# A four-layer image network on one core: the third layer's spectrum layout, token statistics, skip terms and tail rearranged

## The chip, the core and the metric

The kernel runs on one core of one Trainium2 chip. Its metric is the device time of that core in microseconds, from start to end of one launch. The core has four compute engines that work side by side, each through its own list of instructions in order: TensorE (PE; its weight loads are listed as PEld), VectorE (DVE), ScalarE (ACT) and GpSimd (Pool). SyncE (SP) issues the transfers between the chip's memory (HBM) and the core's buffer (SBUF), also in order. TensorE writes its results to PSUM. Engines wait for one another through semaphores.

## What is computed

A batch of four images, each 64 x 64 positions with 128 channels, passes four layers of the form x = x + f(gn(x)), where gn is a group normalisation. The first is a selective scan, the second a Fourier convolution, the fourth a neighbourhood attention; they are not changed. The third is cut here to what matters. It takes each image as t = 64 tokens of H x W = 64 x 128 numbers, and every instance_norm is over one token:

```python
def instance_norm(x, g, b):
    mu = jnp.mean(x, axis=(-2, -1), keepdims=True)
    var = jnp.var(x, axis=(-2, -1), keepdims=True)
    return (x - mu) * jax.lax.rsqrt(var + EPS) * g[:, None, None] + b[:, None, None]

tokens_norm = instance_norm(tokens, norm1_g, norm1_b)
k = fno_layer(tokens_norm, key_w, ..., (Hs, Ws))
q = fno_layer(tokens_norm, query_w, ..., (Hs, Ws))
v = fno_layer(tokens_norm, value_w, ..., (H, W))
...
attn = fno_layer(attn, proj_w, proj_skip_w, proj_skip_b, (H, W))
attn = instance_norm(attn + tokens, attn_norm_g, attn_norm_b)
m = instance_norm(attn, norm2_g, norm2_b)
m = fno_layer(m, mixer_w1, ..., norm=(mixer_norm_g1, mixer_norm_b1), act=_gelu)
m = fno_layer(m, mixer_w2, ..., norm=(mixer_norm_g2, mixer_norm_b2))
out = instance_norm(m, mixer_out_g, mixer_out_b) + attn
```

An fno_layer is a product of a few low Fourier coefficients with weights (norm of that, if one is given) plus a pointwise skip of its input. After the layer, x (its input) is added to out.

## The kernel before

Every image of the third layer lies in SBUF as tiles of 128 partitions x 32 columns j x 128 numbers. A column j holds two tokens, 64 lines each, on the partitions. So a token statistic is one bn_stats per j on DVE (over the 128 numbers of a line) and small TensorE products (in_pm, with the matrices tok and tokM) that sum over the 64 lines.

`layer2` (line 1408) runs the four images through the generator `layer2_image` (line 949), two at a time. `Pace` (line 884) is a planner: it issues the instructions of both images in the order that its own costs give, through `in_turn` (line 922), each generator running until its next `yield`. The order that results is kept on PE, ACT, DVE and Pool; SP takes its transfers in the order of issue. All instructions of the layer are recorded under the planner's call, line 914, so one tells them apart by their tiles.

The large tiles (`xg`, `U2`, `Z2`, `ti`, `z`, `m`, `sp`) share a pool of seven buffers, handed round among both images; a new tile waits for the last reader of the tile whose buffer it takes.

The stages of an image, with the tiles by which the trace names them:

1. Load `xg`, group statistics (`pg`, `gn_st`), normalise, store to a scratch in HBM; token statistics (`in_st`, `in_pm`).
2. The front. `dft_y` (line 1018) transforms the columns: TensorE's `pu`, which ACT copies from PSUM to `U` (line 1025). `U` is the tile `U2`, laid out as token column, real or imaginary component, frequency or row: [P, 64, 2, 32]. Then `px` (line 1139) takes one slice of `U` for each of 32 rows and 2 components as weights, with `quad` as the moving data; `pv` reads eight or fewer rows of `U` as moving data, ACT copies it to `V`, and `pG` (line 1176) multiplies slices of `V` by themselves. Each matrix product of the program has two records in the trace.
3. Attention scores: `TT`, `Z` (two DVE operations and one on Pool per part, three parts), `psc`, softmax in `Sc`, transposed to `PT`; then `pk` applies the value weights to the image in another order of tokens (`ti`), which is written to HBM and read back as `z` (line 1277).
4. `pz`: the two images of a pair meet, and a product with streamed weights (`wr`, `WX`) gives the spectrum `Zp` of both.
5. `synthesis` (line 1029): TensorE's `pa`, an ACT copy to `S`, TensorE's `pb` and then a given `put` for each block of four columns. Here `put` adds to `z` on DVE. When all blocks are done, 32 bn_stats per image read `z` (`token_stats`, line 966), and the factors `sa`, `za`, `A1`, `A2`, `B1` follow.
6. Mixer 1, `spectral` (line 1333): `dft_y` of `z`, `pq` (quad as weights, `U` as moving data), DVE's `Zp` (a product with the mixer weights), synthesis with `put` an ACT copy to `sp`. In the same time DVE makes `m` = `z` x `A2`. Then 32 bn_stats on `sp`, factors `q1` and `f1`, m = gelu(sp x q1 + f1 + m), half of it on ACT and half on DVE.
7. Mixer 2: the same on `m`, into a new `sp`, with 32 bn_stats.
8. The tail: sp x q2, m = m x scal(10) + sp (`stt`, line 1388), x loaded anew into `sp`; 32 bn_stats on `m`; then, per chunk of eight columns, z x sa + f3 on ACT, m x q3 on DVE, the sums with `sp` and `z` on DVE and the store.

`by_rows` (line 1014) is a DVE product or sum of eight columns with one number per partition and column, `affine` (line 1004) is eight ACT instructions of one column each.

Of the kernel before, what the change touches and what calls it, by code (L numbers as in the profile page):

```python
# [17 lines left out]
P = 128  # L18
Q = 68
# [864 lines left out]
class Pace:  # L884


    def __init__(self, nc):
        self.nc, self.free, self.t, self.first = nc, {}, 0.0, None

    def spend(self, name, op, out):  # L890
        n = 1
        for d in out.shape[1:]:
            n *= d
        fixed, each, land = {
            "tensor": (0.02, 0.0017, 0.1),
            "vector": (0.07, 0.00104, 0.1),
            "scalar": (0.17, 0.00083, 0.1),
            "gpsimd": (0.1, 0.0023, 0.1),
            "sync": (0.1, 0.0, 2.0 + n * out.shape[0] * 4e-5),
        }[name]  # L900
        end = max(self.free.get(name, 0.0), self.t) + fixed + each * n
        self.free[name] = end
        self.first = self.first or name
        self.t = end + land

# [43 lines left out]
def layer2_image(sh, w, pools, x_in, x_out, scr, wt, parity, beside):  # L949
# [16 lines left out]
    def token_stats(src):  # L966


        st = own([P, NJ, 6], "in_st")
        for j in range(NJ):  # L970
            nc.vector.bn_stats(st[:, j, :], src[:, j, :])
            if j % 8 == 7:
                yield j == NJ - 1
# [12 lines left out]
        yield True  # L986
        return pm[:, 0, :], pm[:, 1, :]
# [29 lines left out]

    def dft_y(src):

        U = large("U2", [P, 64, 2, 32])  # L1020
        for g in range(NJ // 4):
            pu = ps.tile([P, 4, P], F32, name="pu", tag="a")
            for q in range(4):
                nc.tensor.matmul(pu[:, q, :], lhsT=src[:, 4 * g + q, :], rhs=w["an"], start=True, stop=True)
            nc.scalar.copy(U[:, 8 * g : 8 * g + 8].rearrange("p t q r -> p (t q r)"), pu.rearrange("p q m -> p (q m)"))
            yield g == 7
        return U

    def synthesis(Z, put):
# [20 lines left out]
        for g0 in range(0, 16, 4):  # L1050
            S_next = columns(g0 + 4) if g0 < 12 else None
            for u in range(2):
                pb = ps.tile([P, 4, DM], F32, name="pb", tag="b")
                for q in range(2):
                    nc.tensor.matmul(
                        pb,
                        lhsT=w["bd"][64 * u : 64 * u + 64, q, :],
                        rhs=S[64 * u : 64 * u + 64, :, q, :],
                        start=(q == 0),
                        stop=(q == 1),  # L1060
                    )
                put(u, g0, pb)
            S = S_next
            yield g0 == 12

    def at(t, u, g0):
        return t.rearrange("p (g u) c -> p u g c", u=2)[:, u, g0 : g0 + 4, :]
# [66 lines left out]
    for g in range(8):  # L1134
        px = ps.tile([64, 4, Q], F32, name="px", tag="b")
        for e in range(4):
            for q in range(2):
                nc.tensor.matmul(
                    px[:, e, :], lhsT=U[:, :, q, 4 * g + e], rhs=w["quad"][:, q, :], start=(q == 0), stop=(q == 1)
                )  # L1140
        nc.scalar.activation(Xs[0:64, 4 * g : 4 * g + 4, :], px, AF.Copy, scale=scT[:64])
        if g == 0:
# [22 lines left out]
    for v, r0, r1 in ((1, 0, 8), (2, 8, 9), (0, 9, 16), (3, 16, 17), (0, 17, 24), (1, 24, 32), (None, 0, 0)):  # L1165
        nr = r1 - r0
        if nr:
            V = tmp.tile([66, 64, 8], F32, name="V2", tag="S2", bufs=3)
            pv = ps.tile([66, 64, nr], F32, name="pv", tag="a")
            for q in range(2):  # L1170
                nc.tensor.matmul(pv, lhsT=w["gram"][:, v, q, :], rhs=U[:, :, q, r0:r1], start=(q == 0), stop=(q == 1))
            nc.scalar.copy(V[:, :, :nr], pv)
        if V_last is not None:
            for e in range(V_last[1]):
                Ve = V_last[0][:, :, e]
                nc.tensor.matmul(pG, lhsT=Ve, rhs=Ve, start=(n_done == 0), stop=(n_done == 31))
                n_done += 1
        V_last = V, nr
# [151 lines left out]
    ts(B1, B1, scal(7), scal(9), ALU.add, ALU.add)  # L1330
    yield False

    def spectral(src, mix):
        U = yield from dft_y(src)
        Zm = own([Q, 64, 32], "Zp", tmp)
        for g in range(4):
            px = ps.tile([Q, 16, 32], F32, name="pq", tag="b")
            for q in range(2):
                nc.tensor.matmul(
                    px, lhsT=w["quad"][:, q, :], rhs=U[:, 16 * g : 16 * g + 16, q, :], start=(q == 0), stop=(q == 1)  # L1340
                )
            tt(Zm[:, 16 * g : 16 * g + 16, :], px, mix.unsqueeze(1).to_broadcast([Q, 16, 32]), ALU.mult)
            yield g == 3
        sp = large("sp")
        yield from synthesis(Zm, lambda u, g0, p: nc.scalar.copy(at(sp, u, g0), p))
        return sp


    m = large("m")
    for c in range(4):  # L1350
        by_rows(m, z, A2, c, ALU.mult)
    yield False
    sp = yield from spectral(z, w["mix1"])
    mu, var = yield from token_stats(sp)
    vs = col("vs")
    tt(vs, A1, A1, ALU.mult)
    tt(vs, vs, var, ALU.mult)
# [18 lines left out]
        yield c == 4  # L1376


    sp = yield from spectral(m, w["mix2"])
    mu, var = yield from token_stats(sp)  # L1380
# [10 lines left out]
    mu, var = yield from token_stats(m)  # L1391
    q3 = yield from norm_scale(var, 14, "q3")
    f3 = minus_mean(mu, q3, "f3")
    ts(f3, f3, scal(15), None, ALU.add)
    tt(f3, f3, za, ALU.add)
    yield True
    for n, c in enumerate(C4):
        rows = slice(1024 * n, 1024 * n + 1024)
        affine(z, z, sa, f3, n)
        by_rows(m, m, q3, n, ALU.mult)  # L1400
        tt(m[:, c, :], m[:, c, :], sp[:, c, :], ALU.add)
        yield False
        tt(m[:, c, :], m[:, c, :], z[:, c, :], ALU.add)
        nc.sync.dma_start(x_out[rows, :].rearrange("(j p) d -> p j d", p=P), m[:, c, :])
        yield n == 3

# [467 lines left out]
```

## Time and profile before

| what | us |
|---|---|
| median of the runs | 8041.62 |
| lowest and highest of 3 runs | 8036.29, 8046.07 |
| the profiled execution | 8031.55 |
| its span in the trace | 8029.5 |
| PE busy (share of the span) | 6458.9 (80%) |
| DVE busy | 6721.0 (84%) |
| ACT busy | 6138.5 (76%) |
| Pool busy | 5478.0 (68%) |

The span is the time from the first to the last instruction that the profiler recorded on the core; the profiled execution's own time lies a little above it. Most of the busy time belongs to the first layer, so the shares say little on the third. This is how that layer looks among the costliest groups of instructions (line, engine, operation, tile written and tiles read, shapes and count, then busy us and mean ns of one, then idle time of the engine ahead of the group and what ended it), taken over the window from 6380 to 7480 us:

```profile
L914 PE MATMUL pb<-S,bd 64*128 64x512 f32 x384 | 99.3, 612 | 0.0
L914 PE MATMUL px<-quad,U 128*64 128x68 f32 x512 | 59.6, 284 | 1.4 <-ACT U L914 1.4
L914 ACT COPY U<-pu 128x512 f32<-128x512 f32 x96 | 55.5, 584 | 79.7 <-PE pu L914 79.5
L914 DVE BATCH_NORM_STATS2 in_st<-sp 128x6 f32<-128x128 f32 x256 | 53.5, 277 | 31.6 <-ACT sp L914 31.6
L914 ACT ACTIVATE z<-z,f,sa 128x128 f32<-128x128 f32 x128 | 50.1, 480 | 5.7 <-DVE f L914 5.7
L914 PE MATMUL pG<-V 66*64 66x64 f32 x256 | 36.3, 307 | 0.0
```

Instructions of one engine overlap in their latency, so the mean of one can be longer than the step from one start to the next; of a chain of equal records, the length divided by the count is that step. 128x512 reads as 128 partitions and 512 elements each.

### The profile page before, as it was taken

Reading aid. Unit: us, or ns where it says so; the run is one execution under the profiler, and the core shown is the slowest. Engines: PE = TensorE matmul, PEld = TensorE weight load, DVE = VectorE, ACT = ScalarE, POOL = GpSimd, SP = SyncE. Lnnn points to the kernel's source line nnn. Section 1 sums busy time; section 2 is a strip of 40 time slices with the busy share of each in tenths; the row PEclk is TensorE's granted clock in tenths of the full one; section 3 lists DMA queues with packets and bytes.
Section 4 is the critical chain, followed back from the end, with each engine's and each line's share of the span. In section 5 each row is a group of like instructions: output and inputs, shape, how many; then the busy total and the mean of one; then the engine's idle time right before and its main releaser. Section 6 shows DMA issues by size and latency. Waiting matters only on the chain.

```text
span 8029.5 us, 141288 instructions
## 1 busy us (share of the span) xinstructions
PE 6458.9 (80%) x52976; PEld 4085.6 (51%) x52976; DVE 6721.0 (84%) x7948; ACT 6138.5 (76%) x9798; POOL 5478.0 (68%) x2502
## 2 busy tenths in 40 slices
PE   7688888778888877888887777787778878687789
PEld 3344554444455444445544444454457666464456
DVE  2899999999999999999999999999945545645778
ACT  3799999989999898999999999999822213315567
POOL 0899999998998898899989999999900010020233
PEclk9899999999999999999999999999989978798899
DMA  6446555545655554565655445555542141331332
GB/s 121 163 153 191 170 178 179 161 161 160 193 179 179 173 171 166 164 186 176 185 179 176 161 158 185 176 176 178 174 96 56 42 109 31 90 104 31 105 93 80
DMA packets 1403839, 1165.69 MB, mean 145 GB/s; under 512 B 759829, under 2 KB 1197681, under 8 KB 1336210
## 3 DMA queue, kind: packets, MB, share of 16 engines
q1 hardware_dynamic: 1401474, 1154.93, 46.7%
q8 instruction: 417, 6.83, 0.4%
q14 instruction: 268, 2.20, 0.1%
q10 hardware_dynamic: 1680, 1.74, 0.1%
HBM read 962.66 MB, written 189.74 MB: 144 GB/s over the span
## 4 chain that ended last, share of the span: by engine, by line
PE 35%; ACT 26%; DVE 22%; issue 9%; POOL 4%; DMA 4%; SPq 1%; DVEq 0%; ACTq 0%; POOLq 0%
DVE h L531 13%; ACT hT L401 9%; ACT dA L530 9%; PE pt L391 7%; PE cv L215 6%; PE yT L426 4%; POOL dB L525 2%; ACT e L480 2%; PE po L726 1%; PE pf L721 1%; PE pz L914 1%; PE pt L1557 1%; PE pu L914 1%; DVE in_st L914 1%; ACT delta L333 1%
## 5 line engine op out<-in xcount | busy, mean ns | idle before, releaser
L531 DVE TENSOR_TENSOR_SCAN h<-dA,state,dB 128x512 f32<-128x512 f32 x4096 | 4920.3, 1267 | 219.7 <-POOL dB L525 104.1
L525 POOL TENSOR_TENSOR dB<-du,Bb 128x1024 f32<-128x1024 f32 x2048 | 4808.3, 2385 | 335.7 <-DVE h L531 209.9
L391 PE MATMUL pt<-ident,h 128*128 128x128 f32 x16384 | 2224.7, 279 | 880.8 <-ACT hT L401 874.5
L530 ACT ACTIVATE dA<-delta,A_neg 128x512 f32<-128x512 f32 x4096 | 2767.1, 697 | 197.2 <-DVE h L531 161.6
L391 PEld LDWEIGHTS pt<-ident,h 128*128 128x128 f32 x16384 | 1807.1, 141 | 1923.6 <-ACT hT L401 1721.6
L401 ACT COPY hT<-pt 128x1024 f32<-128x1024 f32 x2048 | 2079.3, 1015 | 157.5 <-PE pt L391 140.1
L426 PE MATMUL yT<-hT,W 128*32 128x256 f32 x16384 | 1380.1, 409 | 1.0 <-ACT hT L401 0.6
L914 POOL COPY XG<-Xs 64x9 f32<-64x9 f32 (+2 forms) x44 | 10.9, 292 | 962.0 <-ACT Xs L914 961.9
L426 PEld LDWEIGHTS yT<-hT,W 128*32 128x32 f32 x16384 | 455.2, 150 | 343.3 <-issue 330.9
L215 PE MATMUL cv<-xn,taps 128*128 128x512 f32 x1152 | 613.2, 633 | 3.5 <-DVE delta L339 3.5
L1595 POOL TENSOR_TENSOR S<-S,sm 128x784 f32<-128x784 f32 x128 | 191.1, 1493 | 432.7 <-DVE sm L1593 257.6
L342 POOL TENSOR_TENSOR du<-delta,u 128x1024 f32<-128x1024 f32 x128 | 304.4, 2378 | 118.2 <-DVE delta L339 118.2
L330 PE MATMUL dp<-xd,w_dt 65*128 65x512 f32 x512 | 289.1, 647 | 71.2 <-ACT Ct L321 43.4
L215 PEld LDWEIGHTS cv<-xn,taps 128*128 128x128 f32 x1152 | 183.7, 189 | 238.0 <-issue 225.0
L313 PE MATMUL xd_ps<-u,w_x 128*48 128x512 f32 x512 | 251.9, 615 | 47.2 <-DMA u<-l_xw 16.3
L1602 ACT ACTIVATE S<-S,mx 128x196 f32<-128x196 f32 x512 | 227.8, 448 | 33.5 <-DVE mx L1629 32.9
L722 ACT ACTIVATE h<-pf,b 128x512 f32<-128x512 f32 x128 | 88.0, 687 | 145.0 <-PE pf L721 145.0
L339 DVE SCALAR_TENSOR_TENSOR delta<-delta,dp 128x512 f32<-128x512 f32 x256 | 170.9, 667 | 26.9 <-ACT delta L336 24.1
L1557 PE MATMUL pt<-ident,S 128*98 128x128 f32 x1024 | 166.1, 287 | 3.3 <-POOL S L1595 1.9
L330 PEld LDWEIGHTS dp<-xd,w_dt 65*128 65x128 f32 x512 | 76.3, 188 | 177.3 <-ACT Ct L321 97.2
L336 ACT ACTIVATE delta<-delta 128x512 f32<-128x512 f32 x256 | 166.3, 650 | 0.1
L333 ACT ACTIVATE delta<-dp 128x512 f32<-128x512 f32 x256 | 153.0, 598 | 10.8 <-PE dp L330 9.9
(344 smaller groups left out, 6829.5 us busy)
## 6 DMA issues: line engine op xcount, KB each, us to landing
Bb<-l_B SPq DMA_DIRECT2D x512, 1024.0 KB
W<-l_W SPq DMA_DIRECT2D x512, 256.0 KB
l_y<-y SPq DMA_DIRECT2D x128, 512.0 KB
u<-l_xw SPq DMA_DIRECT2D x64, 512.0 KB
y<-l_y SPq DMA_DIRECT2D x64, 512.0 KB
u<-l_xr SPq DMA_DIRECT2D x64, 512.0 KB
V<-l_v SPq DMA_DIRECT2D x512, 49.0 KB
wr<-wt SPq DMA_DIRECT2D x128, 136.0 KB
```

The costliest lines, as they stand in the source:

```text
L215: nc.tensor.matmul(pm, lhsT=taps[:, s, t, :], rhs=xn[:, dy : dy + 8, dx : dx + 64], start=(t == 0), stop=(t == 8),)
L313: nc.tensor.matmul(bank["x"], lhsT=w_x[:, s, k, :], rhs=u[:, s, :], start=(s == 0), stop=(s == 1))
L330: nc.tensor.matmul(bank[s], lhsT=w_dt[:, k, s * P : (s + 1) * P], rhs=xd, start=True, stop=True)
L342: nc.gpsimd.tensor_tensor(du, delta, u, ALU.mult)
L391: nc.tensor.transpose(pt[:, j, s, :], G["h"][:, s, t0 : t0 + 32, :].rearrange("p t n -> p (t n)"), sh.ident)
L401: return lambda: nc.scalar.copy(hT, pt.rearrange("p j s d -> p j (s d)"))
L426: nc.tensor.matmul(U["yT"][e][32 * jo : 32 * jo + 32, qo % 2, :], lhsT=U["Ws"][G["g"]][:, :, 4 * q + j], rhs=hT[:, j, :], start=((e, jo) n ...
L525: nc.gpsimd.tensor_tensor(dB, du, B_now[:, q : q + 1, :].to_broadcast([P, 2, CH]), ALU.mult)
L530: nc.scalar.activation(dA, delta[:, s, :], AF.Exp, scale=A_neg[:, k, s, n : n + 1])
L531: nc.vector.tensor_tensor_scan(h[:, s, :, q], dA, dB[:, s, :], state[:, s, n : n + 1], ALU.mult, ALU.add)
L914: r = f(*args, **kw)
L1557: nc.tensor.transpose(pt[:, half, hp, :], U["S"][:, e, hp, 98 * half : 98 * half + 98], sh.ident)
```

## The change

The spectrum tile `U2` is laid out as component, frequency, line. The `U` copy on ACT now writes it strided, `px`, `pv` and `pG` read runs of consecutive elements, and `pq` reads runs of 16 and leaves its result as [frequency, line], which DVE reads transposed. bn_stats of `z` and of `sp` are issued inside the synthesis, four after each block; `aside` keeps the planner from counting their time for the image. The skip terms of the tail move: Pool computes z = z x sa + za + x in place while mixer 1 runs, with x loaded to a new large tile `xr`, and m = m x scal(10) while mixer 2 runs. In the tail m = sp x q2 + m is one DVE instruction per column, with the bn_stats of `m` behind each chunk, and the last step is m x q3 + f3 on ACT and + z on DVE for three chunks of four; the fourth is done on DVE alone.

The diff, cut to its core:

```diff
     def spend(self, name, op, out):
...
         self.free[name] = end
+        if self.aside:
+            return
...
+    def counted(st, src, js):
+        nc.aside = True
+        for j in js:
             nc.vector.bn_stats(st[:, j, :], src[:, j, :])
+        nc.aside = False
...
-        U = large("U2", [P, 64, 2, 32])
+        U = large("U2", [P, 2, 32, 64])
...
-            nc.scalar.copy(U[:, 8 * g : 8 * g + 8].rearrange("p t q r -> p (t q r)"), pu.rearrange("p q m -> p (q m)"))
+            nc.scalar.copy(
+                U.rearrange("p q r t -> p (q r) t")[:, :, 8 * g : 8 * g + 8],
+                pu.rearrange("p j m -> p (j m)").rearrange("p (t k) -> p k t", t=8),
+            )
...
+    def block(u, g0):
+        return range(2 * g0 + u, 2 * g0 + u + 8, 2)
...
-                    px[:, e, :], lhsT=U[:, :, q, 4 * g + e], rhs=w["quad"][:, q, :], start=(q == 0), stop=(q == 1)
+                    px[:, e, :], lhsT=U[:, q, 4 * g + e, :], rhs=w["quad"][:, q, :], start=(q == 0), stop=(q == 1)
...
-            V = tmp.tile([66, 64, 8], F32, name="V2", tag="S2", bufs=3)
-            pv = ps.tile([66, 64, nr], F32, name="pv", tag="a")
+            V = tmp.tile([66, 8, 64], F32, name="V2", tag="S2", bufs=3)
+            pv = ps.tile([66, nr, 64], F32, name="pv", tag="a")
             for q in range(2):
-                nc.tensor.matmul(pv, lhsT=w["gram"][:, v, q, :], rhs=U[:, :, q, r0:r1], start=(q == 0), stop=(q == 1))
-            nc.scalar.copy(V[:, :, :nr], pv)
+                nc.tensor.matmul(pv, lhsT=w["gram"][:, v, q, :], rhs=U[:, q, r0:r1, :], start=(q == 0), stop=(q == 1))
+            nc.scalar.copy(V[:, :nr, :], pv)
...
-                Ve = V_last[0][:, :, e]
+                Ve = V_last[0][:, e, :]
...
-    yield from synthesis(Zp, lambda u, g0, p: tt(at(z, u, g0), at(z, u, g0), p, ALU.add))
-    mu, var = yield from token_stats(z)
+    st = own([P, NJ, 6], "in_st")
+    def added(u, g0, p):
+        tt(at(z, u, g0), at(z, u, g0), p, ALU.add)
+        counted(st, z, block(u, g0))
+    yield from synthesis(Zp, added)
+    mu, var = yield from token_stats(z, st)
...
-            px = ps.tile([Q, 16, 32], F32, name="pq", tag="b")
+            px = ps.tile([Q, 32, 16], F32, name="pq", tag="b")
...
-                    px, lhsT=w["quad"][:, q, :], rhs=U[:, 16 * g : 16 * g + 16, q, :], start=(q == 0), stop=(q == 1)
+                    px, lhsT=w["quad"][:, q, :], rhs=U[:, q, :, 16 * g : 16 * g + 16], start=(q == 0), stop=(q == 1)
...
+        def copied(u, g0, p):
+            nc.scalar.copy(at(sp, u, g0), p)
+            counted(st, sp, block(u, g0))
+            nc.aside = True
+            next(beside, None)
+            nc.aside = False
...
+    def residual():
+        xr = large("xr")
+        load_image(nc, xr, x_in)
+        for n, c in enumerate(C4):
+            wide = lambda v: v[:, c].unsqueeze(2).to_broadcast([P, 8, DM])
+            for v, op in ((wide(sa), ALU.mult), (wide(za), ALU.add), (xr[:, c, :], ALU.add)):
+                nc.gpsimd.tensor_tensor(z[:, c, :], z[:, c, :], v, op)
+            if n % 2:
+                yield
...
+    sp, st = yield from spectral(z, w["mix1"], residual())
...
+    def grown():
+        for n, c in enumerate(C4):
+            nc.gpsimd.tensor_scalar(m[:, c, :], m[:, c, :], scal(10), None, ALU.mult)
+            yield
+
+    sp, st = yield from spectral(m, w["mix2"], grown())
...
-    for n, c in enumerate(C4):
-        if n % 2:
-            by_rows(sp, sp, q2, n, ALU.mult)
-        else:
-            affine(sp, sp, q2, None, n)
-        stt(m[:, c, :], m[:, c, :], scal(10), sp[:, c, :], ALU.mult, ALU.add)
-        nc.sync.dma_start(sp[:, c, :], x_in[1024 * n : 1024 * n + 1024, :].rearrange("(j p) d -> p j d", p=P))
+    st = own([P, NJ, 6], "in_st")
+    for n in range(4):
+        js = range(8 * n, 8 * n + 8)
+        for j in js:
+            stt(m[:, j, :], sp[:, j, :], q2[:, j : j + 1], m[:, j, :], ALU.mult, ALU.add)
+        counted(st, m, js)
         yield n == 3
...
-    tt(f3, f3, za, ALU.add)
...
-        affine(z, z, sa, f3, n)
-        by_rows(m, m, q3, n, ALU.mult)
-        tt(m[:, c, :], m[:, c, :], sp[:, c, :], ALU.add)
-        yield False
-        tt(m[:, c, :], m[:, c, :], z[:, c, :], ALU.add)
+        if n == 3:
+            for j in range(8 * n, 8 * n + 8):
+                stt(m[:, j, :], m[:, j, :], q3[:, j : j + 1], z[:, j, :], ALU.mult, ALU.add)
+            by_rows(m, m, f3, n, ALU.add)
+        else:
+            affine(m, m, q3, f3, n)
+            yield False
+            tt(m[:, c, :], m[:, c, :], z[:, c, :], ALU.add)
         nc.sync.dma_start(x_out[rows, :].rearrange("(j p) d -> p j d", p=P), m[:, c, :])
```

More of the change, by code (lines that the diff above doesn't have):

```diff
@@ L887, in __init__ @@
     def __init__(self, nc):
-        self.nc, self.free, self.t, self.first = nc, {}, 0.0, None
+        self.nc, self.free, self.t, self.first, self.aside = nc, {}, 0.0, None, False
     def spend(self, name, op, out):
@@ L964, in layer2_image, with token_stats @@
     held = lambda shape, name: ps.tile(shape, F32, name=name, tag=f"held{parity}", bufs=1)
-    def token_stats(src):
-        st = own([P, NJ, 6], "in_st")
-        for j in range(NJ):
+    def counted(st, src, js):
+        nc.aside = True
+        for j in js:
             nc.vector.bn_stats(st[:, j, :], src[:, j, :])
-            if j % 8 == 7:
-                yield j == NJ - 1
+        nc.aside = False
+    def token_stats(src, st=None):
+        if st is None:
+            st = own([P, NJ, 6], "in_st")
+            for j in range(NJ):
+                nc.vector.bn_stats(st[:, j, :], src[:, j, :])
+                if j % 8 == 7:
+                    yield j == NJ - 1
         pm = held([P, 2, NJ], "in_pm")
@@ L1331, in layer2_image, with spectral @@
     yield False
-    def spectral(src, mix):
+    def spectral(src, mix, beside=()):
+        beside = iter(beside)
         U = yield from dft_y(src)
@@ L1336, in spectral @@
         for g in range(4):
-            px = ps.tile([Q, 16, 32], F32, name="pq", tag="b")
+            px = ps.tile([Q, 32, 16], F32, name="pq", tag="b")
             for q in range(2):
                 nc.tensor.matmul(
-                    px, lhsT=w["quad"][:, q, :], rhs=U[:, 16 * g : 16 * g + 16, q, :], start=(q == 0), stop=(q == 1)
+                    px, lhsT=w["quad"][:, q, :], rhs=U[:, q, :, 16 * g : 16 * g + 16], start=(q == 0), stop=(q == 1)
                 )
-            tt(Zm[:, 16 * g : 16 * g + 16, :], px, mix.unsqueeze(1).to_broadcast([Q, 16, 32]), ALU.mult)
+            tt(
+                Zm[:, 16 * g : 16 * g + 16, :],
+                px.rearrange("p r t -> p t r"),
+                mix.unsqueeze(1).to_broadcast([Q, 16, 32]),
+                ALU.mult,
+            )
             yield g == 3
         sp = large("sp")
-        yield from synthesis(Zm, lambda u, g0, p: nc.scalar.copy(at(sp, u, g0), p))
-        return sp
+        st = own([P, NJ, 6], "in_st")
+        def copied(u, g0, p):
[4 more added lines that the diff above has]
+            nc.aside = False
+        yield from synthesis(Zm, copied)
+        return sp, st
     m = large("m")
@@ L1352, in layer2_image @@
     yield False
-    sp = yield from spectral(z, w["mix1"])
-    mu, var = yield from token_stats(sp)
+    def residual():
[8 more added lines that the diff above has]
+    sp, st = yield from spectral(z, w["mix1"], residual())
+    mu, var = yield from token_stats(sp, st)
     vs = col("vs")
@@ L1376, in layer2_image @@
         yield c == 4
-    sp = yield from spectral(m, w["mix2"])
-    mu, var = yield from token_stats(sp)
+    def grown():
[3 more added lines that the diff above has]
+    sp, st = yield from spectral(m, w["mix2"], grown())
+    mu, var = yield from token_stats(sp, st)
     q2 = yield from norm_scale(var, 12, "q2")
     yield True
-    for n, c in enumerate(C4):
-        if n % 2:
-            by_rows(sp, sp, q2, n, ALU.mult)
-        else:
-            affine(sp, sp, q2, None, n)
-        stt(m[:, c, :], m[:, c, :], scal(10), sp[:, c, :], ALU.mult, ALU.add)
-        nc.sync.dma_start(sp[:, c, :], x_in[1024 * n : 1024 * n + 1024, :].rearrange("(j p) d -> p j d", p=P))
+    st = own([P, NJ, 6], "in_st")
+    for n in range(4):
[3 more added lines that the diff above has]
+        counted(st, m, js)
         yield n == 3
-    mu, var = yield from token_stats(m)
+    mu, var = yield from token_stats(m, st)
     q3 = yield from norm_scale(var, 14, "q3")
```

## The prediction

> **What bounds the kernel now.** I read the windows by stage first, because the page's shares are means over four layers and the changed layer covers only 6402 to 7460 us. All its work is recorded at L914 (the planner's call), so I go by tiles. It runs two pairs of images, the second 522.2 us after the first; I work out the first and double it. Times that I give for the changed kernel are on this pair's clock, without the front's gain. Columns: window, length, busy us and records of PE, PEld, DVE, ACT, POOL, then clock, DMA share, GB/s.
>
> ```profile
> 6459.00:6553.00 94.00, 90.28 (x696) 76.61 (x696) 29.71 (x72) 24.97 (x48) 15.85 (x26) 0.90 0.17 41
> ...
> 6667.00:6716.00 49.00, 36.71 (x156) 23.96 (x155) 24.41 (x87) 11.70 (x20) 0.00 (x0) 0.87 0.01 4
> 6716.00:6779.00 63.00, 62.28 (x300) 39.70 (x299) 28.23 (x81) 28.48 (x53) 0.00 (x0) 0.97 0.00 1
> 6779.00:6800.00 21.00, 2.33 (x11) 2.33 (x12) 15.88 (x42) 11.57 (x21) 0.00 (x0) 0.56 0.00 1
> 6800.00:6871.00 71.00, 65.66 (x303) 41.49 (x302) 34.98 (x85) 45.03 (x89) 0.00 (x0) 0.94 0.15 41
> 6871.00:6941.00 70.00, 16.58 (x68) 14.33 (x68) 59.72 (x134) 30.44 (x84) 0.00 (x0) 0.54 0.51 139
> ```
>
> The front (first row) and both mixers (third, fifth) are TensorE's. The gelu (fourth) and the tail (sixth) are VectorE's, with ScalarE beside it. Pool does nothing after 6667. The chain of waits (start, length, what) gives the price per record and the breaks:
>
> ```profile
> 6469.31 5.55 PE px L914 x48
> ...
> 6514.96 10.85 PE px L914 x96
> ...
> 6528.60 2.11 PE pG L914 x16
> 6530.70 2.97 PE psc L914 x96
> ...
> 6653.06 14.04 PE pz L914 x224
> ...
> 6699.56 10.85 DVE in_st L914 x56
> 6710.45 5.33 PE in_pm L914 x24
> ...
> 6867.45 6.20 DVE in_st L914 x32
> 6873.70 1.93 PE in_pm L914 x8
> ...
> 6908.88 6.21 DVE in_st L914 x32
> 6915.22 1.90 PE in_pm L914 x8
> ```
>
> A px record costs 5.55/48 = 0.116 us and a pG record 2.11/16 = 0.132, but a pz record, with 68 weight columns where px has 64, 14.04/224 = 0.063. Three times the statistics stand alone on the path.
>
> [...] the groups give 207 ns for px's load and 146 for pz's. [...] px's weights step by 64 elements, pG's by 8, pz's by 1. [...] no run yet varies the step alone. [...] (start, length):
>
> ```profile
> 6523.90 1.22 DVE L914 TENSOR_TENSOR Z<-TT,W 128x1024 f32<-128x1024 f32 x1
> 6524.06 2.81 POOL L914 TENSOR_TENSOR Z<-TT,W 128x1024 f32<-128x1024 f32 x1 [1.34 <-DVE Z L914]
> 6525.15 2.81 DVE L914 TENSOR_TENSOR Z<-Z,Wb 128x1024 f32<-128x1024 f32 x1
> ```
>
> A 1.22 us operation takes 2.81 while Pool works, and Pool too is stretched (its shortest of this kind is 1.90).
>
> **Part 1, layout of U2.** A pair has 256 px records, start to start 112 ns, and 128 pG records at 120. At pz's 62 that is 256×0.050 + 128×0.058 = 12.8 + 7.4 = 20.2 us off TensorE. Not all reaches the end: Z needs about 14.2 us from TT (pT at 6514.2) on DVE and Pool, and now hides under the 96 px and the pG records in front of psc. These shrink by about 6, so psc will wait some 5 us; 15 remain. The lower bound is 0 (step not the cause), the upper 20. The pk stage behind it only shifts. Costs: ScalarE's U copy writes strided. L673, reading PSUM and writing strided, takes 580 ns per 384 elements, and L722 687 per 512 contiguous, the difference of 128 elements at 0.83: no penalty, so I take 0.584 us as now, at worst double (48 copies a pair). Zp reads PSUM transposed: strided DVE rows reach 1.27 us per 512 against 0.685, 8 per mixer and pair, each beside 1.7 us of pq on TensorE; I take 0 (16×0.58 = 9 us per pair if that cover were gone). pq itself reads runs of 16 instead of 32, at 429 ns; pv reads runs of 7 or 8 and takes 1.50/4 us per 448, the same 0.84 ns per element, so 0.
>
> **Part 2, statistics inside the syntheses.** A block of z costs DVE 0.685 + 4×0.19 (bn_stats start every 193 ns) = 1.45 us; TensorE yields two blocks per 3.85. So all fit but the last few, and the stats of both images end about 6702.6 instead of 6712; the inputs of mixer 1's pu come 8.9 us early (bounds 6 and 10). In the mixers the same holds behind each sp copy.
>
> **Part 3, skip terms on Pool.** Per image 4 chunks of three operations. The added input comes at two-input speed, 2.38 us (dB row); the two with a broadcast I price from L1595's 1.493 per 784, i.e. 1.9. So 6.2 per chunk, 24.8 per image, 49.6 per pair; bounds 45 and 70 (all at 2.8). Start about 6714; it stops for xr. Its load goes to the slot of mixer 1's first U2, so it waits for pq, and lands about 6734.5 (the 512 KB image loads took 4.1 to 7.6 us). Both images' xr share a slot: image 0's four loads wait on SP until Pool has finished image 1, about 6756, landing 6760. Behind them on SP stand the next pair's xg loads, which have time. Pool ends 6781 to 6790. Who waits: mixer 2's first U copy on ScalarE takes that slot, at about 6803, 13 us later; queued behind it there are affines and a gelu of image 0. DVE's two-input operations meet Pool: mixer 1's m product (about 3.6 us late, hidden), the small f1 and q1 operations and the gelu's additions (2 to 3 us each time). ScalarE's order also puts f1 and sqrt q1 behind image 0's copies: image 1's m is ready 6798 to 6802, now 6797.2. So part 2's 8.9 us go here (bounds: 0 and 12 given back). Pool's multiplications of m by a scalar (4 per image) come after mixer 2's pu has read m: image 1's 30 us before use, image 0's after 6846.6 (pu in the chain), at most 4×2.38 = 9.5 us, and used after 6871.
>
> **Part 4, mixer 2 and tail.** Image 0's gelu no longer straggles into mixer 2 (done 6813, now 6826), TensorE's 62 us then run closed up: last pb 6864.4 instead of 6870.5, −6 (bounds 0 and −8). In the tail, per pair, go from ScalarE 64 affines of z and 32 of sp, from DVE 8 wide additions of sp, 8 products by q3, 4 by q2 and 2 of the 8 additions of z (22×1.22) and 8 wide scalar_tensor_tensor (1.28), together 37.1 us, and from SP 8 loads. Come 48 affines of m, 64 narrow scalar_tensor_tensor for m, 16 at the end, 2 wide additions of f3. No narrow row exists; L288's 256 elements start every 0.391[...] I take 0.29: 80×0.29 + 2×1.22 = 25.6, DVE's tail is 11.5 shorter (bounds 14 at 0.26, 5 at 0.37). As a check, from image 1's q2 at 6848.5, 4×(8×0.29 + 8×0.2 + 8×0.2 for image 0's stats) = 22.4 gives m's stats at 6871, and the last store about 6918, now 6937; the next pair's first stats end 6923, now 6941.1. So the tail ends 15 to 18 early, of which 6 are mixer 2's; I take 15.
>
> **Sum.** Front 15 + tail 15 = 30 per pair, 8.9 gained and given back; the last pair, followed by the next layer, 14 at the end instead of 15: 59. The profiled execution took 8031.55 us (span 8029.5 and 2.05 around it), so 7972.5. The median of the runs shown is 8041.62, 10 above; less 59 it is 7982.6, which I give. A measurement of this kernel tells apart about 0.2%, 16 us.
>
> **Rivals.**
> - Pool's end holds mixer 2. For it: exclusion is in the trace, two xr loads in series. Against: 13 us of slack. At 2.8 per operation Pool ends about 6812, mixer 2 loses 9 per pair: 59 − 18 = 41, 8001. Chance 0.16.
> - The step is not why px and pG are slow; [...] against: psc's contiguous 64 columns, two halves side by side, at 2.97/96 = 0.031. Gain 59 − 30 = 29, 8013. Chance 0.11.
> - Larger: no collisions at the gelu, so part 2 stays: 59 + 18 = 77, 7965. Chance 0.13.
> - Slower: Pool becomes the bound of mixers and gelu. The last 22 operations start at 6734.5 and have 4 us for the second xr. The gain of 30 per pair is gone when mixer 2 starts at 6833: (6833 − 6738.5)/22 = 4.3 us per operation, as the three operations would reach if DVE's narrow bn_stats or ScalarE excluded Pool too. At 5 us it ends 6848.5, 15 per pair lost: 8042 + 31 = 8073. Against: DVE's scans keep 1267 ns beside a busy Pool and dB is 2385 there. Chance 0.09.
> - My forecast: 0.51.
>
> **How the numbers follow.** The forecast's own spread is about ±18. 7948 below takes in the larger case; 8022 takes in the layout rival; left out are the slower case and a little of each. Of the layout and Pool rivals, 0.09 falls within 0.2% of now. So faster 0.82, same 0.09, slower 0.09.
>
> **What would show it.** px and pG records every 62 ns, front window near 79; in_pm no longer behind in_st at 6699 to 6712; Pool's z rows 1.9 to 2.4, ending before ScalarE's U copies of mixer 2; U copy at 0.58; narrow m operations at 0.26 to 0.29; a tail about 55 long. Wrong if Pool rows reach 4 us, if the U copy doubles, or if m for mixer 2 comes after 6810 less the front's gain.

## The result and the profile after

The changed kernel takes 7971.8 us, the median of four runs (7961.91 to 7974.94), against 8041.93 for the kernel before (8036.29 to 8046.07): a ratio of 0.9911, 95% interval 0.9894 to 0.9928, or 70 us less where 59 were forecast. The profiled execution took 7969.62 us, 61.9 less than the one before; its span is 7967.8. In the two traces the third layer alone, from the first `pg` to the last addition of the tail, went from 1046.1 to 980.3 us, 65.8 less. The layers around it were not edited, and yet what lies ahead of it took 5.1 us longer and what follows it 0.9 less, so stages are compared below inside the layer.

The windows of the changed kernel by stage, cut at the same events as those of before (window, length, busy us and records of PE, PEld, DVE, ACT, POOL, clock, DMA share, GB/s):

```profile
6464.42:6543.42 79.00, 68.33 (x696) 54.86 (x696) 29.49 (x73) 24.70 (x48) 15.83 (x26) 0.91 0.20 49
6661.26:6701.11 39.85, 36.86 (x153) 22.96 (x153) 25.07 (x85) 11.52 (x19) 0.00 (x0) 0.94 0.01 5
6701.11:6763.83 62.72, 62.70 (x301) 40.36 (x301) 36.07 (x100) 27.22 (x50) 38.67 (x19) 0.96 0.27 68
6763.83:6796.36 32.53, 7.77 (x37) 7.02 (x36) 25.23 (x37) 21.17 (x43) 15.13 (x7) 0.62 0.00 1
6796.36:6858.03 61.67, 60.57 (x276) 37.85 (x276) 30.18 (x109) 30.00 (x52) 20.80 (x7) 0.95 0.13 35
6858.03:6909.15 51.12, 10.90 (x49) 10.25 (x48) 39.76 (x142) 20.12 (x52) 0.00 (x0) 0.52 0.41 113
```

The front is 79 long and was 94. Pool is now busy through mixer 1 and the gelu (third and fourth rows). The fourth row, from the last pb of mixer 1 to the first U copy of mixer 2, is the one that grew. VectorE's work in the tail (last row) fell from about 60 to 40.

The groups of the same layer (window 6380 to 7420; out<-in, shapes, count, busy us, mean ns, then idle time ahead of it and what ended it):

```profile
L916 POOL TENSOR_SCALAR m<-m,scal 128x1024 f32<-128x1024 f32 x16 | 48.1, 3012 | 68.3 <-PE pu L916 38.5 <-ACT sp L916 22.3 <-ACT m L916 7.5
L916 POOL TENSOR_TENSOR z<-z,xr 128x1024 f32<-128x1024 f32 x16 | 37.6, 2348 | 32.2 <-DMA xr<-x 31.2
L916 PE MATMUL px<-quad,U 128*64 128x68 f32 x512 | 34.8, 231 | 1.4 <-ACT U L916 1.4
L916 PEld LDWEIGHTS px<-quad,U 128*64 128x64 f32 x512 | 33.2, 144 | 2.1 <-ACT U L916 1.7
L916 DVE TENSOR_TENSOR Zp<-pq,mix 68x512 f32<-68x512 f32 x32 | 21.7, 682 | 45.1 <-PE pq L916 45.1
L916 PE MATMUL pG<-V 66*64 66x64 f32 x256 | 19.7, 227 | 0.1
```

px's busy time fell from 59.6 to 34.8 and pG's from 36.3 to 19.7; their weight loads are at 144 ns, pz's value. Zp's transposed read of PSUM costs nothing (682 ns, before 685), and the strided U copy neither (585, before 584). Pool's two additions took 2.01 us (za, a broadcast) and 2.35 (x) in the mean, where 1.9 and 2.38 were assumed. Its multiplication of m by one scalar, with one tensor input, takes 3.0 us: more than the 2.38 that I had called its upper bound.

The stages, in us, from the times of the events in the two traces (first pair, second pair):

| stage | before | after |
|---|---|---|
| first pu of xg to first pk | 93.8, 97.7 | 79.0, 86.9 |
| first pk to last pz | 114.4, 114.6 | 117.8, 113.8 |
| last pz to last pb of z | 31.8, 31.8 | 33.0, 33.0 |
| last pb of z to first pu of z | 16.8, 16.8 | 6.8, 6.5 |
| first pu of z to last pb of mixer 1 | 62.7, 62.7 | 62.7, 62.1 |
| last pb of mixer 1 to first U copy of mixer 2 | 23.2, 23.2 | 32.5, 32.6 |
| first U copy to last pb of mixer 2 | 69.0, 69.0 | 61.7, 61.3 |
| last pb of mixer 2 to last addition | 67.3, 65.7 | 51.1, 51.1 |

In the chain of waits of the changed kernel (start, length, what) the statistics of z no longer stand ahead of in_pm, which starts 3.4 us after the last pb and did so after 11.6, and the front has a new wait, Z on Pool ahead of psc:

```profile
6507.94 2.94 POOL Z L916
...
6516.37 2.81 POOL Z L916
6521.67 4.76 PE psc L916 x92
...
6697.68 3.62 PE in_pm L916 x16
```

### The profile page after: what moved, and what is told of

Read it like the earlier page. It is cut to its first block, busy times and chain, and to the rows that moved or that the text cites. A ratio compares the mean times of both kernels' runs of the same rounds, so it can differ in the third digit from the quotient of the medians.

```text
span 7967.8 us, 141369 instructions
## 1 busy us (share of the span) xinstructions
PE 6423.2 (81%) x52976; PEld 4046.1 (51%) x52976; DVE 6716.4 (84%) x8048; ACT 6102.2 (77%) x9698; POOL 5629.2 (71%) x2566
## 4 chain that ended last, share of the span: by engine, by line
PE 35%; ACT 25%; DVE 22%; issue 9%; POOL 4%; DMA 4%; SPq 1%; DVEq 0%; ACTq 0%; POOLq 0%
DVE h L531 13%; ACT hT L401 9%; ACT dA L530 9%; PE pt L391 7%; PE cv L215 6%; PE yT L426 4%; POOL dB L525 2%; ACT e L480 2%; PE po L726 1%; PE pf L721 1%; PE pz L916 1%; PE pu L916 1%; PE pt L1609 1%; POOL du L342 1%; ACT delta L333 1%
## 5 line engine op out<-in xcount | busy, mean ns | idle before, releaser
L313 PE MATMUL xd_ps<-u,w_x 128*48 128x512 f32 x512 | 250.1, 611 | 47.3 <-DVE gn_st L171 16.2
L916 POOL TENSOR_TENSOR WX<-wr,Xs 128x544 f32<-128x544 f32 x40 | 59.6, 1491 | 148.4 <-issue 63.3
```

The source lines that it names most:

```text
L313: nc.tensor.matmul(bank["x"], lhsT=w_x[:, s, k, :], rhs=u[:, s, :], start=(s == 0), stop=(s == 1))
L916: r = f(*args, **kw)
```

## Experiments

My theory after the first comparison: the gain is three separate pieces (layout, statistics, tail), and the loss ahead of mixer 2 comes from two things that act one behind the other: small VectorE operations that wait for whole Pool operations, and the U copies' place in ScalarE's order. The rivals: Pool's end holds mixer 2; strided reads are not what the layout mended; parts 1 and 2 hide each other. The second half of the theory, the place of the U copies, did not hold as the cause of the loss; part 2 alone shows what was.

### Part 1 alone

The edit is the layout of U2 and V2 with their readers, on the kernel before.

> The kernel before with part 1 alone (U2 and V2 laid out with the line last). My theory: the step of the weight reads is the cause, so px and pG records start every 59 to 62 ns as in the changed kernel, the U copy stays at 0.585 us and Zp at 0.69; the front from the first pu of xg to the first pk is 15 us shorter in the first pair and 11 in the second, nothing else moves: 8042 less 26 = 8016. Rival (layout pays back in the mixers by strided PSUM reads or pq's shorter runs): pq above 429 ns or the mixers longer by 5 us or more, and 8030 or above.

Measured: 8020.5 us, ratio 0.9975 (0.9965 to 0.9984). px's records fell to 35.4 us in all, the front took 80.5 and 87.3 us (13.3 and 10.4 less), pq and Zp stayed at their prices (610 ns in the mean, before 619, and 685 as before). The layer's stretch is 18 us shorter, where I expected 26: mixer 2 of the first pair took 3.3 us more, and the stage from the first pk to the last pz 1.7 and 1.1; why was not traced. That the layout sets the price of px holds (35.4 us for 512 records, before 59.6), but the gain is smaller than expected.

### Part 2 alone

The edit is `counted`, `aside` and the two `put` functions with their statistics, on the kernel before.

> The kernel before with part 2 alone (bn_stats of z and sp inside the syntheses, not counted by the planner). My theory: the break between the synthesis of z and mixer 1 shrinks from 16.8 to about 6.8 us per pair, 10 each; between mixer 1 and mixer 2 the statistics no longer stand on the path (another 5 to 10 per pair, if the order on ScalarE does not give it back), and the tail is unchanged: 20 to 40 us less in all, I say 8042 - 28 = 8014. Rival (the gain at z is given back at the gelu even without Pool, because ScalarE's order changes with the planner's clock): the stretch from the last pb of mixer 1 to the first U copy of mixer 2 grows from 23 to 32 us, and the time is 8030 or above.

Measured: 8015.1 us, 0.9971 (0.9959 to 0.9982), the layer 21.5 us shorter. The break before mixer 1 is 6.8 and 6.2 us. From the last pb of mixer 1 to the first U copy it takes 27.7 us in both pairs, 4.5 more than before, and from there to the last pb of mixer 2 it takes 61.2 and 62.6 instead of 69. So about half of what the changed kernel loses before mixer 2 comes without any Pool work.

Where it is lost can be read from the first affine of the gelu (ScalarE's sp x q1 + f1). Before, it follows the last sp copy at once:

```profile
6778.32 0.58 ACT L914 COPY sp<-pb 128x512 f32<-128x512 f32 x1 [0.35 <-PE pb L914]
6778.80 3.18 ACT L914 ACTIVATE sp<-sp,f,q 128x128 f32<-128x128 f32 x8
```

With part 2 alone it waits for VectorE's f:

```profile
6772.76 0.63 PE L916 MATMUL in_pm<-in_d,tok 128*128 128x32 f32 x4
...
6775.96 1.64 DVE L916 BATCH_NORM_STATS2 in_st<-sp 128x6 f32<-128x128 f32 x8 [0.84 <-ACT sp L916]
6777.52 0.17 DVE L916 TENSOR_TENSOR vs<-A 128x32 f32<-128x32 f32 x1
...
6780.53 3.18 ACT L916 ACTIVATE sp<-sp,f,q 128x128 f32<-128x128 f32 x8 [2.19 <-DVE f L916]
```

The statistics of the image that is ahead are complete on TensorE at 6773.4, but the small operations that make its f1 (from vs on) stand in VectorE's order behind the last bn_stats of the other image, which wait for that image's sp copies. So the first affine starts 5.1 us after the last pb of mixer 1; before it was 0.5, in the changed kernel it is 9.9. From the first affine to the first U copy all three take 22.7 us. The whole loss therefore lies ahead of the gelu, in the chain to f1, and not in the place of the U copies. That the planner's not counting the bn_stats put the chain there is likely, but no run tests it.

### Parts 1 and 2 together

> The kernel before with parts 1 and 2 together, without the moved skip terms and the fused tail. The two alone took 18 and 21 us off the layer's stretch in their traces. My theory: they lie in different stages and add up, 39 to 41 less, 8001; what is missing to the changed kernel's 70, about 27 in two pairs, is parts 3 and 4, and lies in the tail, from the last pb of mixer 2 to the last addition (66 to 67 us before, 51 after). Rival: parts 1 and 2 hide each other (less than 30 together, 8010 or more).

Measured: 7989.3 us, 0.9938 (0.9924 to 0.9953), the layer 45.8 us shorter. They add up and a little more (the 3.3 us of mixer 2 are gone). To the changed kernel 20 us of the layer are missing. They are parts 3 and 4: the tail takes 66.5 and 66.0 us here and 51.1 there, a gain of 15 per pair, while the stretch before mixer 2 takes 27.7 and 28.0 here and 32.5 there, a loss of 4.7. The moved skip terms and the fused operations of the tail were not run apart from each other.

### Without Pool's skip terms

```diff
-            for v, op in ((wide(sa), ALU.mult), (wide(za), ALU.add), (xr[:, c, :], ALU.add)):
-                nc.gpsimd.tensor_tensor(z[:, c, :], z[:, c, :], v, op)
+            nc.gpsimd.tensor_tensor(z[:, c, 0:1], z[:, c, 0:1], xr[:, c, 0:1], ALU.add)
```

> The changed kernel with Pool's three wide operations per chunk cut to one narrow one (1 column number of 128; the scaling of z and the addition of x are thereby left out; the loads of x stay). My theory: Pool never holds mixer 2 (it ended 20 us before the first U copy), it costs only through the small DVE operations ahead of the gelu that wait for a whole Pool operation each, about 5.5 us per pair: 7972 - 11 = 7961, and the stretch from the last pb of mixer 1 to the first U copy of mixer 2 shrinks from 32.5 to about 27. Rival (Pool's end or its hold on DVE is what keeps mixer 2 back by the 9 us): that stretch falls to 20 to 23, and the time to 7950 or less. Other rival: no change, 7972.

Measured: 7958.3 us, 0.9899 (0.9884 to 0.9915). The stretch is 27.73 us in both pairs, 4.8 less, and the same as with part 2 alone. The timelines of VectorE and of Pool in the changed kernel show what it was (start, length):

```profile
6765.97 1.40 DVE L916 TENSOR_TENSOR vs<-A 128x32 f32<-128x32 f32 x1
6767.47 0.19 DVE L916 TENSOR_TENSOR vs<-vs,in_pm 128x32 f32<-128x32 f32 x1
...
6767.84 1.98 DVE L916 TENSOR_TENSOR in_d<-in_d 128x64 f32<-128x64 f32 x1
6769.74 0.34 DVE L916 RECIPROCAL q<-q 128x32 f32<-128x32 f32 x1
6770.12 1.51 DVE L916 TENSOR_SCALAR q<-q,scal 128x32 f32<-128x32 f32 x1
...
6772.11 1.54 DVE L916 TENSOR_TENSOR f<-f,B 128x32 f32<-128x32 f32 x1
```

```profile
6765.43 1.89 POOL L916 TENSOR_TENSOR z<-z,za 128x1024 f32<-128x1024 f32 x1
6767.40 2.34 POOL L916 TENSOR_TENSOR z<-z,xr 128x1024 f32<-128x1024 f32 x1
6769.70 1.90 POOL L916 TENSOR_TENSOR z<-z,sa 128x1024 f32<-128x1024 f32 x1
6771.67 1.94 POOL L916 TENSOR_TENSOR z<-z,za 128x1024 f32<-128x1024 f32 x1
```

And VectorE's same operations with Pool idle:

```profile
6763.21 0.17 DVE L916 TENSOR_TENSOR vs<-A 128x32 f32<-128x32 f32 x1
6763.48 0.19 DVE L916 TENSOR_TENSOR vs<-vs,in_pm 128x32 f32<-128x32 f32 x1
...
6764.74 0.22 DVE L916 TENSOR_TENSOR in_d<-in_d 128x64 f32<-128x64 f32 x1
...
6765.26 0.24 DVE L916 TENSOR_SCALAR q<-q,scal 128x32 f32<-128x32 f32 x1
...
6765.99 0.19 DVE L916 TENSOR_TENSOR f<-f,B 128x32 f32<-128x32 f32 x1
```

Four operations of 0.2 us take 1.4 to 2.0 each, and each ends within 0.1 us of the end of the Pool operation of that moment (6767.37 and 6767.32, 6769.82 and 6769.74, 6771.63 and 6771.59, 6773.66 and 6773.61). The operation with an input from PSUM (vs<-vs,in_pm) and the reciprocal fall into a Pool operation too and don't wait (0.19 and 0.34 us, the same as with Pool idle). The tensor_scalar does, though it has one tensor input (1.51 us beside 0.24). Why the one waits and the other doesn't, the traces don't show.

### More Pool work

```diff
-            for v, op in ((wide(sa), ALU.mult), (wide(za), ALU.add), (xr[:, c, :], ALU.add)):
+            for v, op in (
+                (wide(sa), ALU.mult),
+                (wide(za), ALU.add),
+                (xr[:, c, :], ALU.add),
+                (xr[:, c, :], ALU.subtract),
+                (xr[:, c, :], ALU.add),
+            ):
```

> The changed kernel with two more wide Pool operations per chunk (x subtracted and added again), 16 per pair at 2.34, 37.5 us more of Pool per pair. Pool ended 20 us before the first U copy of mixer 2 in the first pair and 20 in the second. My theory: the cover is those 20 us, what goes beyond is paid in full: Pool ends at about 37.5 later, mixer 2's first U copy waits for it and comes 17 us later per pair, 7972 + 35 = 8007, still faster than before. Rival (Pool's hold on VectorE counts for more than its end): the gelu's additions wait for Pool all along and the loss is 25 us per pair or more, 8022 or above. Other rival (slack larger than read): 7980 or less.

Measured: 8030.3 us, 0.9992 (0.9985 to 0.9999), the layer 58.5 us longer than the changed kernel's, 29 per pair: my 17 was too little, and by its number the first rival came true (8022 or above). One of VectorE's wide operations in the gelu, then ScalarE's last gelu ahead of the U copies and the first of these, then Pool's end:

```profile
6797.74 3.35 DVE L916 TENSOR_TENSOR sp<-sp,q 128x1024 f32<-128x1024 f32 x1
```

```profile
6813.37 1.06 ACT L916 ACTIVATE m<-m 128x1024 f32<-128x1024 f32 x1 [4.83 <-DVE m L916]
6822.14 1.56 ACT L916 COPY U<-pu 128x512 f32<-128x512 f32 x3 [7.71 <-POOL z L916]
```

```profile
6812.33 9.77 POOL L916 TENSOR_TENSOR z<-z,xr 128x1024 f32<-128x1024 f32 x3
```

VectorE's wide operations took 1.22 us in the gelu of the changed kernel and take mostly about 3 here (3.35 in the line shown). So the last gelu ahead of the U copies ends 55.5 us after the last pb of mixer 1, where it ended after 32.6: that is 23 of the 31 us by which the stretch to the first U copy grew, and it is what the rival said of the gelu. The other 8 are Pool's end, for which the copy waits: the prediction's rival "Pool's end holds mixer 2", brought about. In the changed kernel Pool ended at 6776.03 and the copy began at 6796.36, so the cover there was 20.3 us. Pool pays as well: three of its additions take 9.77 us in the gelu and 7.2 in the mixer, so the added 37.5 us became 51. The price of Pool work depends on the stage that it runs into.

### The step of the weights

```diff
-                nc.tensor.matmul(pG, lhsT=Ve, rhs=Ve, start=(n_done == 0), stop=(n_done == 31))
+                Ve, Vm = V_last[0][:, e, :], V_last[2][:, e // step, :, e % step]
+                if weights:
+                    Ve, Vm = Vm, Ve
+                nc.tensor.matmul(pG, lhsT=Ve, rhs=Vm, start=(n_done == 0), stop=(n_done == 31))
```

> The changed kernel with a second copy of V, from which pG takes one of its two operands: in the first pair image 0 reads weights with a step of 2 elements (8 bytes) and image 1 with 4 (16 bytes), in the second pair image 0 reads weights with a step of 8 (32 bytes) and image 1 reads its moving data with a step of 8, its weights contiguous. pG records now start every 58 ns, before (both at step 8) every 120. [...] 58 at step 2, about 115 at 4 and 8; the moving data at step 8 costs nothing (pv's strided moving read took the same per element as pk's), 58. Rival A: any step over 1 costs, 115 at step 2 too. Rival B: the moving data is what cost, 58, 58, 58 and 115. The time itself is not what this run is for (more ScalarE copies).

The time of this kernel is 7972.6 us (one run). Of each image the first run of 16 pG records in TensorE's timeline, in the order weights at step 2, 4, 8, then moving data at step 8:

```profile
6489.69 1.17 PE L916 MATMUL pG<-V 66*64 66x64 f32 x16
...
6514.67 2.13 PE L916 MATMUL pG<-V 66*64 66x64 f32 x16 [0.25 <-ACT V L916]
...
6982.15 2.13 PE L916 MATMUL pG<-V 66*64 66x64 f32 x16
...
7012.41 2.08 PE L916 MATMUL pG<-V 66*64 66x64 f32 x16 [0.47 <-ACT V L916]
```

In the changed kernel such a run takes 1.15 us, in the kernel before 2.18. Step 2 is free (1.17 us), step 4 takes 1.85 times as long as contiguous weights (2.13), step 8 no longer than step 4 (2.13). That the difference would lie between 2 and 4 was an assumption of mine; what makes it the run doesn't show. I was wrong on the moving data: at step 8 with contiguous weights it costs nearly the same (2.08 us), and both strided together (the kernel before, 2.18) cost hardly more than one. pv with 7 or 8 rows was no counterexample: its moving reads took runs of as many consecutive elements in the kernel before, and its four records of 448 or 512 elements take 1.67 and 1.88 us before and after. The pv with one row (128x64), which I had overlooked, reads its moving data at step 64 in the kernel before and in one run in the changed one: its records start every 112 ns before and every 60 after.

### The U copies earlier

In the gelu loop of mixer 1, for the image with parity 1 (the core of the edit):

```diff
+        if c == 2 and parity:
+            U = large("U2", [P, 2, 32, 64])
+        if c > 1 and parity:
+            dft_step(U, m, 2 * c - 4)
+            dft_step(U, m, 2 * c - 3)
```

> The changed kernel with the pu products and U copies of mixer 2 of the image that is ahead issued inside the gelu loop, one chunk behind each gelu, so that on ScalarE they no longer stand behind affines and a gelu of the other image. My theory: the 9 us lost between mixer 1 and mixer 2 are ScalarE's order: the first U copy comes about 15 us earlier, the last of that image's eight about 8, mixer 2 and the tail move up by 8 per pair: 7972 - 16 = 7956. Rival (Pool, or VectorE, holds mixer 2): the U copies come earlier but mixer 2's last pb does not move, 7972. A third way: the other image's gelu is now late by the 4.7 us of the copies and the tail waits for it, 7975 or more.

Measured: 7976.0 us, 0.9928 (0.9915 to 0.994), no better than the changed kernel; the layer takes 986.6 us, 6 more. In the first pair the first U copy came 13 us earlier (19.4 after the last pb of mixer 1) and the ahead image's statistics 7, but the last pb of mixer 2 did not: TensorE's timeline shows it behind another product.

```profile
6855.02 1.99 PE L916 MATMUL pb<-S,bd 64*128 64x512 f32 x8
6861.28 1.06 PE L916 MATMUL in_pm<-in_st,tok 128*128 128x32 f32 x4 [4.27 <-DVE in_st L916]
...
6863.13 3.39 PE L916 MATMUL pb<-S,bd 64*128 64x512 f32 x8
```

TensorE stood 4.3 us with a pb in hand, because the planner had put the statistics product of the other image ahead of it. Two of its costs can explain that: a narrow VectorE operation of 128 elements is 0.07 + 128 × 0.00104 = 0.20 us to it, where the trace has one every 0.262, and the bn_stats of m behind each chunk it does not count for the image at all. In the second pair the image with parity 0 was ahead, so the edit helped the wrong one: the tail there takes 59.7 us instead of 51.1.

### The same for the image that is ahead, and its in_pm after the last pb

`ahead` is the image that reaches its gelu first in its pair; it takes the U copies as above. The bn_stats of m are issued without `aside` as well. The rest of the edit:

```diff
+    if ahead:
+        yield lambda: beside.count("mix2") == 2
     mu, var = yield from token_stats(m, st)
```

> The earlier U copies again, but for the image that is ahead in both pairs (the run before gave them in the second pair to the image behind), and with the statistics products of the ahead image's m put on TensorE after the other image's last pb. In the run before, in pair one, the ahead image had its first pq 6.3 us and its statistics 7.2 us earlier, and then TensorE stood 4 us with the other image's last pb behind an in_pm that waited for VectorE. My theory: both orders are the planner's, not a resource's; with both mended the ahead image is 6 to 7 us earlier through mixer 2 and its tail, the last pb 4 to 6 earlier, the end of the pair 5 to 7: against the changed kernel 10 to 14 less, 7972 - 12 = 7960. Rival: VectorE's work from the gelu to the tail is the bound, and the pair ends where it did: 7972 within 3.

Measured: 7951.8 us, 0.9897 (0.9882 to 0.9913); the layer takes 971.8 us. From the last pb of mixer 1 to the last pb of mixer 2 it takes 89.6 us in both pairs, where the changed kernel takes 94.2 and 93.9, and from there to the last addition 49.3 and 49.6 instead of 51.1. The chain to f1 is no earlier: the first affine still starts 9.9 and 9.8 us after the last pb of mixer 1. What fell is the way from it to the first U copy, from 22.7 to 9.7 us. So the order of issue won time back, at another place than where it had been lost. The edit's three pieces (the copies, the place of in_pm, the counting of m's statistics) were not run apart.

### za in f3, alone and with the order

z's shift za needs no Pool operation: it can go into f3, as it did before the change.

```diff
-            for v, op in ((wide(sa), ALU.mult), (wide(za), ALU.add), (xr[:, c, :], ALU.add)):
+            for v, op in ((wide(sa), ALU.mult), (xr[:, c, :], ALU.add)):
...
     ts(f3, f3, scal(15), None, ALU.add)
+    tt(f3, f3, za, ALU.add)
```

> The changed kernel once more, unedited, beside the next two on the same chip: 7972, about 0.991 of before. It is the mark for them.

> The changed kernel with the addition of za taken out of Pool's three operations per chunk and into the factor f3 of the tail (one small VectorE operation per image), 8 Pool operations of 1.9 us less per pair. My theory from the run without Pool's operations: the loss before the gelu is the small VectorE operations between 6766 and 6774 that wait for Pool; Pool now ends about 12 us earlier, ahead of them, so the stretch from the last pb of mixer 1 to the first U copy falls from 32.5 to 27.7 us, 4.8 per pair: 7972 - 10 = 7962, 9 us less in the layer's own stretch of 980. Rival: the second xr load, not Pool's count, sets Pool's end, which then moves by 5 us or less; nothing gained, 7972.

> The same edit on top of the kernel with the earlier U copies and the mended order on TensorE. My theory: the two gains lie one behind the other, in the chain to f1 and in ScalarE's order after it, and add up: 980 - 9 - 9 = 962 us of the layer's stretch, 7972 - 18 = 7954. Rival: the gelu is bound by ScalarE and VectorE together, so that the start that is won is lost in their work: no better than the kernel with the order alone (972 us of stretch).

Measured on one chip: the changed kernel 7966.1 us, 0.9906 (0.9892 to 0.9921), its layer 978.2; with za in f3 7963.2, 0.9905 (0.9888 to 0.9921), its layer 971.0; with both 7950.4, 0.9882 (0.9865 to 0.99), its layer 961.6. With za in f3 Pool ends 2.7 us before the last pb of mixer 1, not 12.2 after it, and the stretch to the first U copy is 28.3 and 27.9 us; by whole runs this edit alone can't be told from the changed kernel. Together with the order the layer is 962 us as forecast: the two gains lie one behind the other, ahead of the first affine (now 6.0 and 5.6 us after the last pb) and between it and the first U copy (9.7 us). What part 2 costs through the place of the chain to f1 is still in it. The last kernel has the shortest layer of all that were run. The layer's stretch tells it from the changed kernel (962 against 978 and 980); by whole runs the two intervals overlap.

ScalarE's timeline of the changed kernel, and below it of the last one, shows what the order moved:

```profile
6792.34 3.17 ACT L916 ACTIVATE sp<-sp,f,q 128x128 f32<-128x128 f32 x8
6795.42 1.04 ACT L916 ACTIVATE m<-m 128x1024 f32<-128x1024 f32 x1
6796.36 1.52 ACT L916 COPY U<-pu 128x512 f32<-128x512 f32 x3
```

```profile
6780.85 1.04 ACT L916 ACTIVATE m<-m 128x1024 f32<-128x1024 f32 x1
6781.80 1.04 ACT L916 COPY U<-pu 128x512 f32<-128x512 f32 x2
```

Above, three U copies whose pu were done at 6785.4 stand behind gelus and affines, some of them of the other image; below they come two by two behind their own gelu (the first two are shown).

## Why the prediction was right, step by step

- **Part 1, 15 per pair.** The front gave 14.8 and 10.8. px and pG start every 59 and 58 ns, the forecast 62. As forecast, part of TensorE's gain went to a wait for Z: PE's idle time ahead of psc grew from 6.5 to 13.7 us over four images, 3.6 per pair where I had put 5. But the stage behind it did not only shift: up to the last pz the gain is 11.4 and 11.6 (in the second trace of the changed kernel 14.0 and 9.5), some 23 us in two pairs where I had 30. Where the rest goes was not tested.
- **Part 2, 8.9 per pair, given back before mixer 2.** The break shrank by 9.9 and 10.2, the synthesis itself took 1.3 more: 8.6 and 8.9. The stretch to the first U copy grew by 9.3 and 9.4, all of it ahead of the gelu's first affine. Both causes that I had named were there: collisions with Pool are 4.8 of it (run without the skip terms), and image 1's factors behind image 0's last blocks the other 4.5 (part 2 alone). I had these behind image 0's copies on ScalarE; they stand behind its statistics on VectorE, which wait for those copies. Taken as an edit, though, part 2 is not worth nothing: alone it shortens the layer by 21.5 us, since only half of that loss is there and mixer 2 closes up with it (69.0 us to 61.2 and 62.6), which I had entered under part 4.
- **Part 3.** Undisturbed, Pool's prices were 1.89 for the broadcasts and 2.35 for x; it ended at 6776.0, which on the prediction's clock is 6781.8 (the last pz came 5.8 us earlier than before), the early end of 6781 to 6790. The first U copy came at 6802.2 on that clock, forecast 6803, so the cover was 20.3 us; my 13 was reckoned from the late end. The narrowest point is not Pool's end but the chain to f1.
- **Part 4, mixer 2.** Forecast 6 earlier from the synthesis of z on; measured in the first pair 9.9 − 1.3 − 2.1 = 6.5, with 2.1 for the way from the first pu of z to the last pb of mixer 2 (154.9 to 156.9); in the second pair 7.8.
- **Part 4, tail: the term that was too small.** From the last pb to the last addition I had 15 − 6 = 9 per pair; it gave 16.2 and 14.6. Two of its numbers were off. The narrow operations start every 0.262 us, close to an estimate from the trace of before: L288's 0.391 us for 256 elements less 128 at 1.05 ns (685 ns for 512 elements, 1222 for 1024) is 0.257. No row of that trace showed the 0.29 that I took: 80 × 0.028 = 2.2 us. And I left all 32 statistics of the trailing image's sp in the tail; in the window of the tail 16 are left, 16 × 0.2 = 3.2. By these sums that is 5.4 of the 5.6 to 7.2 us missing per pair; no run isolates it. (In the check of this term, 4 × (2.32 + 1.6 + 1.6) is 22.1, not 22.4.)
- **The sum.** Against 59, the layer gained 65.8 us in the two traces. The terms missed with opposite signs: the front gave 7 us less than forecast over both pairs, mixer 2 and the tail 15 more, and the gap from the first pair's last addition to the second pair's first pu grew by 1.8. That the sum came so near is in part luck. The rest of the 70 lies outside the layer or between executions: the medians differ by 70.1, the two profiled executions by 61.9.

Of the rivals, the step was why px and pG were slow (part 1 alone, px 59.6 us before and 35.4 after; the step of the weights, 16 pG records in 1.15 us contiguous and 2.13 at a step of 4 or 8). By its number the rival "larger" (77) is a little nearer to 70 than the forecast; the trace speaks against it, since the collisions at the gelu were there and part 2's gain of the break was lost ahead of it. In the changed kernel Pool did not hold mixer 2, nor did it become the bound. The run with more Pool work shows that this danger was real: at 40 wide operations on z per pair instead of 24, only some 8 of the 70 us are left (8030.3 against 8038.8).

## What to carry to other kernels

Where TensorE reads an operand of fp32 with a step and the record is short, look at the start-to-start time against a contiguous record of that size. Here 16 pG records took 2.13 us with weights at a step of 4 or 8, 2.08 with moving data at 8, and 1.17 with weights at 2, where contiguous ones took 1.15; px's records, weights at 64, started every 112 ns and contiguous every 59, and those of the pv with one row, moving data at 64, every 112 and 60. The repair can be a layout that another engine writes at no cost (here ScalarE's copy, 585 ns after and 584 before). Work given to an idle Pool is priced not by its end alone but also by the short VectorE operations of a dependent chain that run beside it (here four of 0.2 us became 1.4 to 2.0), and by the wide ones (1.22 us became about 3, 3.35 in the line shown); move it away from them, or shorten it, before adding more. Look also at what a chain stands behind in its engine's order: work moved forward from one image can hold the other image's chain. And when a planner orders instructions, an operation that it counts too cheaply, or not at all, shows up as an engine that waits with ready work behind the head of its queue.

## What was not expected of the hardware

Pool's tensor_scalar of 128x1024 with a scalar per partition takes 2.84 us at least and 3.0 in the mean, longer than its two-input addition of the same size (2.35) and its product with a broadcast (1.89). A moving operand with a step of 8 elements slows a pG record as much as weights with that step, and the two together hardly further (2.08, 2.13 and 2.18 us for 16 records, contiguous 1.15). VectorE's reading of PSUM at a step of 16 elements costs nothing (682 ns for 512, before 685).
